# Order of the attention products in each unit, and the two ends of a spatial self-attention kernel

## The chip, the cores and the metric

The kernel runs on one core of a Trainium2 chip. The metric is the device time of one execution in microseconds (us). The kernel before takes 2449.17 us, the median of 10 executions (2448.07 to 2451.79).

## What is computed

The reference is self-attention over the 4096 positions of each of four images, with raw reshapes: the projections are made per position, and then the (position, channel) block of each image is read anew as (channel, position).

```
q = x @ Wq + bq        # x: (4, 64, 64, 256), q and k: 128 channels
k = x @ Wk + bk
v = x @ Wv + bv        # 256 channels
pq, pk, pv = reshape of q, k, v to (B, channels, N), N = 4096
energy = einsum('bcn,bcm->bnm', pq, pk)
attention = softmax(energy, axis=-1)
out = einsum('bcm,bnm->bcn', pv, attention)
y = gamma * out.reshape(x.shape) + x          # float32
```

## The kernel before

**Tiling.** Each image has 32 row blocks of 128 keys (`NM` = 32) and 16 groups of 256 queries (`NG` = 16). A group is worked off in eight units (`NU` = 8), and a unit holds four key blocks. So there are 4 x 16 x 8 = 512 units. In the loop at the end of the fast part, `u` counts an image's 128 units, and `g, t = divmod(u, NU)` gives the group and the unit's place `t` in it.

**Split numbers.** The products run on 32-bit tiles of the type float32r, and each factor is split into an upper part and rests, so that three products stand for one. For the energies (`energy`, L330) a unit has 12 products of 256 columns: 8 into `sa` and 4 into `sb`. ACT takes their exponentials into `x` and `y` (L334), DVE multiplies these (`join`, L344), ACT makes the upper part `h` (`upper`, L349), and DVE makes `l` and `d` (`halves`, L355 and L358). Then `attend` (L383) adds the unit's share of the output: `h` times `vh`, `l` times `vl`, `d` times `vd`, eight products for each pair, in this order. I call the three sets of eight **phases h, l and d**.

**The products of a phase.** The stationary operand is a block of the unit's own tile, `left[:, i, j * P : (j + 1) * P]`, with `i` = 0 to 3 for the key block and `j` = 0 or 1 for the half of the 256 queries. The moving operand is the value block `right[:, m, :]` with

```
m = 2 * t + i // 2 + NI * (i % 2)
```

that is `m` = 2t, 2t+16, 2t+1, 2t+17 for `i` = 0 to 3. In `vh` and `vl` a value block has 256 channels, two columns of ones that sum the softmax's denominator, and two columns of padding: the products move 258 columns, and the blocks lie 260 x 4 = 1040 bytes apart. In `vd` there are 256 columns, 1024 bytes apart. Phases h and l add into the PSUM tiles `a0` and `a1` (one for each `j`, each in a bank of its own), phase d into `bb` (both `j` in one bank). The order in a phase is `j` outermost and `i` inside, upwards; only in phase l, for `j` = 1 and `t` = 1 or 3, `i` runs downwards (`back`).

**Order of the work.** The schedule is written out by hand (`manual_schedule`): energies of unit u + 3, `join` and `upper` of u + 2, `halves` of u + 1, `attend` of u. So an engine's instructions run in the order in which the loop issues them. After the last unit of a group ACT copies the two sums out of PSUM (L394), and `finish` scales, transposes and adds `x` some units later. The next group's sums use the same PSUM tiles.

**The start.** ACT's queue issues the two loads of `Wq` and `Wk` (L90, L91) first; ACT then loads its activation table and writes the ones into `vh` and `vl` (L224). SP's queue loads the blocks of `x` (L82), POOL's queue the biases, `Wv`, `bv` and `gamma`. PE runs 12 transposes of the identity tile into a scratch tile `wp` (L199), whose result nobody reads; the identity tile is made by POOL. Then it transposes the first two blocks of `x` (L124) and projects the first (L137).

**The end.** `finish_last` handles the last group of the last image. DVE copies the two denominators (L447), `factors` takes reciprocals and multiplies by gamma (L399, L400), L450 makes the second factor; `guard` checks that all denominators lie in a safe range (L431 to L439), piece by piece between the other steps. For each half, ACT scales `bb` out of PSUM (L455), DVE adds the scaled sum to it (L458), PE transposes (L463), DVE adds `x` (L468), and SP stores (L469). The value that `guard` leaves in `again` decides whether a slower general version runs; in these executions it doesn't.

Of the kernel before, what the change touches and what calls it, by code (L numbers as in the profile page):

```python
# [9 lines left out]
F32 = mybir.dt.float32  # L10
F32R = mybir.dt.float32r
I32 = mybir.dt.int32
AF = mybir.ActivationFunctionType
ALU = mybir.AluOpType
AX = mybir.AxisListType
# [5 lines left out]
def kernel(  # L21
# [36 lines left out]
    nc = tc.nc  # L58
    B, W, H, C = x.shape
    P = 128  # L60
    N = W * H
    C2 = C // 2
    NM = N // P
    KC = C // P
    NI = NM // 2
# [19 lines left out]
    ident = const.tile([P, P], F32, name="ident")  # L85
    make_identity(nc, ident)
    ones = const.tile([P, P], F32, name="ones")
    nc.vector.memset(ones, 1.0)
    wqk_sb = const.tile([P, KC, 2 * C2], F32, name="wqk_sb")
    nc.scalar.dma_start(wqk_sb[:, :, :C2], wq.rearrange("(k p) d -> p k d", p=P))  # L90
    nc.scalar.dma_start(wqk_sb[:, :, C2:], wk.rearrange("(k p) d -> p k d", p=P))  # L91
    bqk_sb = const.tile([P, 2 * C2], F32, name="bqk_sb")
    nc.gpsimd.dma_start(bqk_sb[:, :C2], bq.partition_broadcast(P))
    nc.gpsimd.dma_start(bqk_sb[:, C2:], bk.partition_broadcast(P))
# [6 lines left out]
    gam, gam1 = gam2[:, :1], gam2[:, 1:]  # L101
# [73 lines left out]
    NB = 256  # L175
    NJ = NB // P
    NG = N // NB
    NU = NM // 4
# [3 lines left out]
    E = 2.0**-12  # L182
# [4 lines left out]
    again = const.tile([P, 1], I32, name="again")  # L187
    zs = const.tile([P, 1], F32, name="zs")

    zall = const.tile([P, B * NG, NJ], F32, name="zall")  # L190
# [4 lines left out]

    with tc.tile_pool(name="ps_w", bufs=1, space=PSUM) as ps_w:
        wp = ps_w.tile([P, P], F32, name="wp")
        for _ in range(12):
            nc.tensor.transpose(wp, ident, ident)  # L199

    with ExitStack() as fast:
        fast.enter_context(tc.manual_schedule())
# [6 lines left out]
        ppool = pool("ppool", 2)  # L209
        pool("pad2", 1).tile([P, 112], F32, name="pad2")  # L210
        work = pool("work", 2)
# [3 lines left out]
        ps_s = pool("ps_s", 2, space=PSUM)  # L215
        ps_o = pool("ps_o", 1, space=PSUM)
        ps_t = pool("ps_t", 1, space=PSUM)


        vh = qkv.tile([P, NM, VC], F32R, tag="vh", name="vh")  # L220
        vl = qkv.tile([P, NM, VC], F32R, tag="vl", name="vl")
        vd = qkv.tile([P, NM, C], F32R, tag="vd", name="vd")
        for t in (vh, vl):
            nc.scalar.copy(t[:, :, C : C + 2], ones[:, : 2 * NM].rearrange("p (m t) -> p m t", t=2))  # L224

        images, qd, kf, units, loads, now = [], {}, {}, {}, {}, {}

# [124 lines left out]
        def halves(b, u):  # L352
# [7 lines left out]
            )  # L360
            units[b, u] = h, l, d

        def attend(b, u):

            g, t = divmod(u, NU)
            if t == 0:
                now["acc"] = [
                    ps_o.tile([P, C + 2], F32, tag=f"a{j}", name=f"a{j}_{b}_{g}")
                    for j in range(NJ)
                ]  # L370
                now["bb"] = ps_o.tile([P, NJ, C], F32, tag="bb", name=f"bb_{b}_{g}")
            h, l, d = units[b, u]
            acc, bb = now["acc"], now["bb"]
            for left, right in ((h, vh), (l, vl), (d, vd)):
                for j in range(NJ):
                    out_ = bb[:, j, :] if left is d else acc[j]


                    back = left is l and j == NJ - 1 and t in (1, 3)
                    for i in reversed(range(4)) if back else range(4):  # L380
                        m = 2 * t + i // 2 + NI * (i % 2)

                        nc.tensor.matmul(  # L383
                            out_,
                            left[:, i, j * P : (j + 1) * P],
                            right[:, m, : out_.shape[1]],
                            start=(t == i == 0 and (left is h or left is d and j == 0)),
                            stop=(t == NU - 1 and i == 3 and left is not h),
                            skip_group_check=True,
                        )  # L390
            if t == NU - 1 and (b, g) != (B - 1, NG - 1):
                o = now["o"] = work.tile([P, NJ, C + 2], F32, tag="o", name=f"o_{b}_{g}")
                for j in range(NJ):
                    nc.scalar.activation(o[:, j, :], acc[j], AF.Identity, scale=1.0 + E)  # L394

        def factors(b, g, gamma):

            r = work.tile([P, 2, NJ], F32, tag="r", name=f"r_{b}_{g}")
            nc.vector.reciprocal(r[:, 0, :], zall[:, b * NG + g, :])  # L399
            nc.vector.tensor_tensor(r[:, 0, :], r[:, 0, :], gamma.to_broadcast([P, NJ]), ALU.mult)  # L400
            return r[:, 0, :], r[:, 1, :]

        def finish(b, g, o, bb, xr):
            yield
            yield

            nc.vector.tensor_copy(zall[:, b * NG + g, :], o[:, :, C])
            r, _ = factors(b, g, gam1)
            nc.vector.tensor_tensor(o[:, :, :C], o[:, :, :C], bb, ALU.add)
            yield  # L410
            for j in range(NJ):
                nc.scalar.activation(
                    o[:, j, :C], o[:, j, :C], AF.Identity, scale=r[:, j : j + 1]
                )
            yield
            yield
            tp = ps_t.tile([P, 2, NB], F32, tag="t", name=f"ot_{b}_{g}")
            for s in range(2):
                for j in range(NJ):
                    nc.tensor.transpose(  # L420
                        tp[:, s, j * P : (j + 1) * P], o[:, j, s * P : (s + 1) * P], ident
                    )
            yield
            nc.vector.tensor_tensor(xr, xr, tp, ALU.add)
            nc.gpsimd.dma_start(ov[b, g], xr)

        def guard():

            z = zall.rearrange("p n j -> p (n j)")
            ok = ppool.tile([P, 4, NB], F32, tag="y", name="ok")[:, 0, : B * NG * NJ]  # L430
            nc.vector.tensor_scalar(ok, z, Z_LOW, None, ALU.is_ge)  # L431
            nc.vector.scalar_tensor_tensor(ok, z, Z_HIGH, ok, ALU.is_le, ALU.mult)
            yield
            nc.vector.tensor_reduce(zs, ok, AX.X, ALU.min)
            nc.vector.tensor_scalar(zs, zs, 0.5, None, ALU.is_lt)
            zp = ps_s.tile([P, 1], F32, tag="b", name="zp")
            nc.tensor.matmul(zp, ones, zs, start=True, stop=True)
            yield
            nc.vector.tensor_copy(again, zp)  # L439
            yield  # L440
            yield

        def finish_last(b, g, xr):

            for j in range(NJ):
                a = now["acc"][j]
                nc.vector.tensor_copy(zall[:, b * NG + g, j : j + 1], a[:, C : C + 1])  # L447
            r, ra = factors(b, g, gam)
            check = guard()
            nc.vector.tensor_scalar(ra, r, 1.0 + E, None, ALU.mult)  # L450
            o = work.tile([P, NJ, C + 2], F32, tag="o", name=f"o_{b}_{g}")
            tps = []
            for j in range(NJ):
                next(check)
                nc.scalar.activation(  # L455
                    o[:, j, :C], now["bb"][:, j, :], AF.Identity, scale=r[:, j : j + 1]
                )
                nc.vector.scalar_tensor_tensor(  # L458
                    o[:, j, :C], now["acc"][j][:, :C], ra[:, j : j + 1], o[:, j, :C], ALU.mult, ALU.add
                )  # L460
                tp = (ps_t, ps_s)[j].tile([P, 2, P], F32, tag="ta"[j], name=f"ot_{b}_{g}_{j}")
                for s in range(2):
                    nc.tensor.transpose(tp[:, s, :], o[:, j, s * P : (s + 1) * P], ident)  # L463
                tps.append(tp)
            for j in range(NJ):
                next(check)
                n = slice(j * P, (j + 1) * P)
                nc.vector.tensor_tensor(xr[:, :, n], xr[:, :, n], tps[j], ALU.add)  # L468
            nc.sync.dma_start(ov[b, g], xr)  # L469
# [19 lines left out]
        for b in range(B):  # L489
            pr = images[b]  # L490
            if b == 0:
                now["banks"] = energies
                pr.transposed(0)
                pr.transposed(1)
                project_qk(b, 0)
            for i in range(1, NI):
# [13 lines left out]
            for u in range(STEPS):  # L510
                g, t = divmod(u, NU)
# [47 lines left out]
    NB = 512  # L559
    NG = N // NB  # L560
    NJ = NB // P
    NP = NM // 2
    xg, og = columns(x, NB), columns(out, NB)
    with tc.If(nc.values_load(again[0:1, 0:1]) > 0), ExitStack() as general:
# [4 lines left out]
        ppool, work = pool("gp", NP + 2), pool("gw", 1)  # L569
        ps_s = pool("gs", 2, space=PSUM)  # L570
        ps_t = pool("gt", 2, space=PSUM)
        ps_o = pool("go", 1, space=PSUM)
        for b in range(B):
# [16 lines left out]
            for g in range(NG):  # L590
                ps = []
                mx = work.tile([P, 2, NB], F32, tag="mx", name=f"gmx_{b}_{g}")
                for t in range(NP):
                    sp = ps_s.tile([P, 2, NB], F32, tag="s", name=f"gs_{b}_{g}_{t}")
                    for h in range(2):
# [4 lines left out]
                            start=True,  # L600
                            stop=True,
                        )
                    p = ppool.tile([P, 2, NB], F32, tag="p", name=f"gp_{b}_{g}_{t}")
# [7 lines left out]
                for j in range(NJ):  # L611
# [17 lines left out]
                acc = [  # L629
                    ps_o.tile([P, NB], F32, tag=f"o{s}", name=f"go{s}_{b}_{g}")  # L630
                    for s in range(2)
                ]
# [60 lines left out]
```

## Time and profile before

| | |
|---|---|
| median of 10 executions | 2449.17 us |
| the profiled execution | 2448.89 us |
| its span, first to last instruction | 2447.1 us |
| PE busy | 2434.0 us, 19,982 products |
| DVE busy | 2100.0 us |
| ACT busy | 1795.3 us |
| POOL busy | 424.6 us |
| DMA | 498.92 MB, mean 204 GB/s |

The profile is of one execution. PE is the engine of the matrix products, PEld its loads of the stationary operand, DVE the vector engine, ACT the engine of the activation functions, POOL the general one, SP the one that only issues transfers here. A line of a group of instructions gives the source line, the engine, the operation, the tiles (out<-in), the shapes, how many there were, their busy time, the mean length of one in ns, and the idle time ahead of them with what ended it. A product's length in the records is longer than the distance to the next one, because the products are pipelined; where I speak of the pace of products I use the distance from start to start.

### The profile page before, as it was taken

The numbers are of one execution on the slowest core, as the hardware profiler recorded it, in microseconds if no ns is written. First come the engines' busy times: TensorE is split into PE (matmuls) and PEld (weight loads), VectorE is DVE, ScalarE is ACT, GpSimd is POOL, SyncE is SP. The second block draws the span as 40 slices with busy tenths as digits, with TensorE's granted clock in tenths as the row PEclk, the third lists the DMA queues.
The fourth block names the chain that finished last, engine by engine and source line by source line (L and its number), as shares of the span: only waits on it lengthen the run. The fifth ranks groups of instructions, "written<-read, shape, count | busy, mean of one in ns | idle before, by whom it ended". The sixth has DMA issues, their size and how long they took to land.

```text
span 2447.1 us, 50024 instructions
## 1 busy us (share of the span) xinstructions
PE 2434.0 (99%) x19982; PEld 2403.2 (98%) x19982; DVE 2100.0 (86%) x2314; ACT 1795.3 (73%) x3201; POOL 424.6 (17%) x781
## 2 busy tenths in 40 slices
PE   9999999999999999999999999999999999999998
PEld 8999999999899999999989999999998999999998
DVE  5988888888698888888869888888886988888887
ACT  5777777777677777777667777777766777777775
POOL 4211111111411111111141111111114111111110
PEclk9999999999999999999999999999999999999999
DMA  7766666665776666666477666666647766666663
GB/s 232 221 203 212 205 205 201 205 213 157 231 224 198 209 206 206 207 198 212 145 241 228 202 203 206 206 211 201 206 141 246 227 204 201 206 207 211 203 202 112
DMA packets 137407, 498.92 MB, mean 204 GB/s; under 512 B 15536, under 2 KB 57264, under 8 KB 137168
## 3 DMA queue, kind: packets, MB, share of 16 engines
q0 software_dynamic: 92320, 453.17, 59.6%
q1 hardware_dynamic: 44304, 42.22, 5.5%
q8 instruction: 160, 2.62, 0.4%
q14 instruction: 79, 0.65, 0.1%
q10 hardware_dynamic: 544, 0.26, 0.0%
HBM read 445.25 MB, written 50.33 MB: 203 GB/s over the span
## 4 chain that ended last, share of the span: by engine, by line


## 5 line engine op out<-in xcount | busy, mean ns | idle before, releaser
L334 ACT ACTIVATE x<-sa 128x512 f32<-128x512 f32 x1024 | 612.3, 598 | 510.2 <-PE sa L330 508.0
L344 DVE TENSOR_TENSOR x<-x,y 128x1024 f32<-128x1024 f32 x512 | 626.9, 1224 | 228.4 <-ACT y L334 228.4
L330 PE MATMUL sa<-q,k 128*128 128x256 f32 x4096 | 733.6, 279 | 0.0
L358 DVE SCALAR_TENSOR_TENSOR d<-h,x 128x1024 fp32r<-128x1024 f32 x512 | 624.3, 1219 | 0.0
L355 DVE TENSOR_TENSOR l<-x,h 128x1024 fp32r<-128x1024 f32 x512 | 624.0, 1219 | 0.0
L330 PEld LDWEIGHTS sa<-q,k 128*128 128x128 f32 x4096 | 618.1, 188 | 0.7 <-ACT y L334 0.2
L334 ACT ACTIVATE y<-sb 128x512 f32<-128x512 f32 x1024 | 616.2, 602 | 0.0
L383 PE MATMUL a<-vh,h 128*128 128x258 f32 x4096 | 574.6, 283 | 0.0
L383 PE MATMUL a<-vl,l 128*128 128x258 f32 x4096 | 572.2, 282 | 0.0
L330 PE MATMUL sb<-q,k 128*128 128x256 f32 x2048 | 567.2, 277 | 0.0
L383 PE MATMUL bb<-vd,d 128*128 128x256 f32 x4096 | 556.7, 278 | 0.0
L314 POOL DMA_DIRECT2D k<-kf x512 | 278.8, 545 | 1568.1 <-PE sb L330 1535.7
L349 ACT ACTIVATE h<-x 128x1024 fp32r<-128x1024 f32 x512 | 544.2, 1063 | 8.6 <-DVE x L344 8.0
L383 PEld LDWEIGHTS a<-vl,l 128*128 128x128 f32 x4096 | 524.6, 189 | 0.0
L383 PEld LDWEIGHTS a<-vh,h 128*128 128x128 f32 x4096 | 522.8, 190 | 0.0
L383 PEld LDWEIGHTS bb<-vd,d 128*128 128x128 f32 x4096 | 513.6, 188 | 0.0
L330 PEld LDWEIGHTS sb<-q,k 128*128 128x128 f32 x2048 | 385.1, 188 | 0.1
L137 PE MATMUL qk<-wqk_sb,xts 128*128 128x256 f32 x512 | 121.1, 379 | 0.0
L158 PE MATMUL v<-xts,wv_sb 128*128 128x256 f32 x512 | 120.3, 380 | 0.0
L158 PEld LDWEIGHTS v<-xts,wv_sb 128*128 128x128 f32 x512 | 97.5, 190 | 13.0
L137 PEld LDWEIGHTS qk<-wqk_sb,xts 128*128 128x128 f32 x512 | 92.5, 190 | 9.8
L275 POOL DMA_DIRECT2D qd<-qks x128 | 69.3, 549 | 179.5 <-DVE qks L146 170.3
(56 smaller groups left out, 865.3 us busy)
## 6 DMA issues: line engine op xcount, KB each, us to landing
k<-kf POOLq DMA_DIRECT2D x512, 768.0 KB, 4.6
x<-in_x_dram SPq DMA_DIRECT2D x128, 256.0 KB, 3.9
kf<-f POOLq DMA_DIRECT2D x64, 384.0 KB, 3.9
out_dram<-x POOLq DMA_DIRECT2D x63, 256.0 KB, 2.6
qd<-qks POOLq DMA_DIRECT2D x128, 64.0 KB, 2.9
qr<-qd SPq DMA_DIRECT2D x64, 128.0 KB, 3.6
wv_sb<-in_L_conv_Wv_dram POOLq DMA_DIRECT2D x1, 256.0 KB, 6.7
out_dram<-x SPq DMA_DIRECT2D x1, 256.0 KB, 3.6
```

Source lines behind the costliest of these rows:

```text
L137: nc.tensor.matmul(qk[:, s, :], self.xt[i][:, k, s, :], wqk_sb[:, k, :], start=(k == 0), stop=(k == KC - 1),)
L158: nc.tensor.matmul(vp[:, eh, :], wv_sb[:, k, eh * P : (eh + 1) * P], self.xt[i][:, k].rearrange("p s a -> p (s a)"), start=(k == 0), stop= ...
L275: nc.gpsimd.dma_start(qd[b, i // 2 + NG // 2 * s][:, i % 2, :], x[:, s, :C2])
L314: nc.gpsimd.dma_start(t.rearrange("p (i s) f d -> p i s (f d)", s=2), kf[b, u % NU])
L330: nc.tensor.matmul(to[:, i], kt[:, 2 * k + i, f, :], q[:, f], start=first, stop=last)
L334: nc.scalar.activation(to[:, 2 * k : 2 * k + 2, :], sp.rearrange("p i j d -> p i (j d)"), AF.Exp, scale=scale,)
L344: nc.vector.tensor_tensor(x, x, y, ALU.mult)
L349: nc.scalar.activation(h, units[b, u], AF.Identity, scale=UPPER)
L355: nc.vector.tensor_tensor(l, x, h.bitcast(F32), ALU.subtract)
L358: nc.vector.scalar_tensor_tensor(d, h.bitcast(F32), 1.0 + E, x, ALU.mult, ALU.subtract)
L383: nc.tensor.matmul(out_, left[:, i, j * P : (j + 1) * P], right[:, m, : out_.shape[1]], start=(t == i == 0 and (left is h or left is d and ...
```

## The change

It has four parts.

1. The two loads of `Wq` and `Wk` are issued by ACT's queue after the two writes of ones into `vh` and `vl`, and so after the table load.
2. PE's idle products at the start are 7 plain products of the tile of ones (which DVE writes with a memset) in place of 12 transposes of the identity; and 2 more stand between the transposes of the first and the second block of `x`.
3. In phases h and l the eight products run in an order that a table gives for each `t` and phase; a digit is 4j + i. Phase d runs as before, `01234567`. The flag `start`, which begins a sum in a PSUM bank, is set at the first product into each bank, whichever it is.
4. In `finish_last` ACT scales the sums out of `a0` and `a1`, each with its own factor, and DVE adds the scaled `bb`; before, it was the other way round. The range check of all but the last group's denominators is done ahead, that of the last group's two after their factors, and `again` is written with a comparison between the two halves. `factors` and `guard` are gone; `finish` has the lines of `factors` in it.

```diff
-    nc.scalar.dma_start(wqk_sb[:, :, :C2], wq.rearrange("(k p) d -> p k d", p=P))
-    nc.scalar.dma_start(wqk_sb[:, :, C2:], wk.rearrange("(k p) d -> p k d", p=P))
...
-        for _ in range(12):
-            nc.tensor.transpose(wp, ident, ident)
+        for _ in range(7):
+            nc.tensor.matmul(wp, ones, ones, start=True, stop=True)
...
         for t in (vh, vl):
             nc.scalar.copy(t[:, :, C : C + 2], ones[:, : 2 * NM].rearrange("p (m t) -> p m t", t=2))
+        nc.scalar.dma_start(wqk_sb[:, :, :C2], wq.rearrange("(k p) d -> p k d", p=P))
+        nc.scalar.dma_start(wqk_sb[:, :, C2:], wk.rearrange("(k p) d -> p k d", p=P))
...
+        ORDERS = (
+            ("13564072", "14325076"),
+            ("41256307", "41763502"),
+            ("26147053", "35601472"),
+            ("41236075", "57104632"),
+            ("10436572", "10726543"),
+            ("57164203", "34250167"),
+            ("35042176", "65341027"),
+            ("35210467", "15347062"),
+        )
+
+        def order(f, b, g, t):
+            return "01234567" if f == 2 else ORDERS[t][f]
...
-            for left, right in ((h, vh), (l, vl), (d, vd)):
-                for j in range(NJ):
+            begun = set()
+            for f, (left, right) in enumerate(((h, vh), (l, vl), (d, vd))):
+                for n, x in enumerate(order(f, b, g, t)):
+                    j, i = divmod(int(x), 4)
                     out_ = bb[:, j, :] if left is d else acc[j]
-                    back = left is l and j == NJ - 1 and t in (1, 3)
-                    for i in reversed(range(4)) if back else range(4):
-                        m = 2 * t + i // 2 + NI * (i % 2)
-                        nc.tensor.matmul(
-                            out_,
-                            left[:, i, j * P : (j + 1) * P],
-                            right[:, m, : out_.shape[1]],
-                            start=(t == i == 0 and (left is h or left is d and j == 0)),
-                            stop=(t == NU - 1 and i == 3 and left is not h),
-                            skip_group_check=True,
-                        )
+                    bank = 2 if left is d else j
+                    m = 2 * t + i // 2 + NI * (i % 2)
+                    nc.tensor.matmul(
+                        out_,
+                        left[:, i, j * P : (j + 1) * P],
+                        right[:, m, : out_.shape[1]],
+                        start=(t == 0 and bank not in begun),
+                        stop=(t == NU - 1 and n >= 6 and left is not h),
+                        skip_group_check=True,
+                    )
+                    begun.add(bank)
...
+        def inside(ok, z):
             nc.vector.tensor_scalar(ok, z, Z_LOW, None, ALU.is_ge)
             nc.vector.scalar_tensor_tensor(ok, z, Z_HIGH, ok, ALU.is_le, ALU.mult)
...
+            inside(ok[:, 0, :n0], z[:, :n0])
+            nc.vector.tensor_reduce(last[:, NJ:], ok[:, 0, :n0], AX.X, ALU.min)
+            acc, bb = now["acc"], now["bb"]
+            for j in range(NJ):
+                zj, raj = z[:, n0 + j : n0 + j + 1], r[:, 1, j : j + 1]
+                nc.vector.tensor_copy(zj, acc[j][:, C : C + 1])
+                nc.vector.reciprocal(r[:, 0, j : j + 1], zj)
+                nc.vector.tensor_tensor(raj, r[:, 0, j : j + 1], gam1, ALU.mult)
+                nc.scalar.activation(o[:, j, :C], acc[j][:, :C], AF.Identity, scale=raj)
+            nc.vector.tensor_tensor(r[:, 0, :], r[:, 0, :], gam.to_broadcast([P, NJ]), ALU.mult)
+            inside(last[:, :NJ], z[:, n0:])
+            nc.vector.tensor_reduce(zs, last, AX.X, ALU.min)
             zp = ps_s.tile([P, 1], F32, tag="b", name="zp")
             nc.tensor.matmul(zp, ones, zs, start=True, stop=True)
             tps = []
             for j in range(NJ):
                 nc.vector.scalar_tensor_tensor(
-                    o[:, j, :C], now["acc"][j][:, :C], ra[:, j : j + 1], o[:, j, :C], ALU.mult, ALU.add
+                    o[:, j, :C], bb[:, j, :], r[:, 0, j : j + 1], o[:, j, :C], ALU.mult, ALU.add
                 )
...
+                if j == 0:
+                    nc.vector.tensor_scalar(again, zp, P - 0.5, None, ALU.is_lt)
...
                 pr.transposed(0)
+                wp = ps_t.tile([P, P], F32, tag="t", name="wp1")
+                for _ in range(2):
+                    nc.tensor.matmul(wp, ones, ones, start=True, stop=True)
                 pr.transposed(1)
```

## Prediction

> **What bounds the kernel now.** I read the page's head first, then the groups of instructions, then the timeline of one unit, of the last unit, of the first 9 us and of the last 4.
>
> ```profile
> PE 2434.0 (99%) x19982; PEld 2403.2 (98%) x19982; DVE 2100.0 (86%) x2314; ACT 1795.3 (73%) x3201; POOL 424.6 (17%) x781
> PEclk9999999999999999999999999999999999999999
> ```
>
> PE has no gaps to speak of and its clock is full in every slice. So the time is the number of products times their pace, and the ends. DVE is next, with 14% to spare.
>
> ```profile
> L330 PE MATMUL sa<-q,k 128*128 128x256 f32 x4096 | 733.6, 279 | 0.0
> L383 PE MATMUL a<-vh,h 128*128 128x258 f32 x4096 | 574.6, 283 | 0.0
> L383 PE MATMUL a<-vl,l 128*128 128x258 f32 x4096 | 572.2, 282 | 0.0
> L383 PE MATMUL bb<-vd,d 128*128 128x256 f32 x4096 | 556.7, 278 | 0.0
> L344 DVE TENSOR_TENSOR x<-x,y 128x1024 f32<-128x1024 f32 x512 | 626.9, 1224 | 228.4 <-ACT y L334 228.4
> ```
>
> No group of products has idle time ahead of it. DVE even waits 228.4 us for ACT, and ACT in turn for PE's energies: both follow PE. One unit in the timeline (columns: start, length, engine):
>
> ```profile
> 401.38 0.39 PE L330 MATMUL sa<-q,k 128*128 128x256 f32 x2
> ...
> 402.74 1.12 PE L383 MATMUL a<-vh,h 128*128 128x258 f32 x8
> 403.70 1.12 PE L383 MATMUL a<-vl,l 128*128 128x258 f32 x8
> 404.65 1.09 PE L383 MATMUL bb<-vd,d 128*128 128x256 f32 x8
> 405.58 0.39 PE L330 MATMUL sa<-q,k 128*128 128x256 f32 x2
> ```
>
> Twelve energies take 1.36 us from start to start (113.3 ns each), phase h 0.96, l 0.95, d 0.93: 4.20 us a unit. 512 units are 2150 us of the 2447. Two columns more than 256 should cost 2/256 of 113.3, 0.9 ns, so 114.2 ns a product; h and l take 119.6. The last unit, with nearly all else at rest, goes at the same pace:
>
> ```profile
> 2433.71 1.13 PE L383 MATMUL a<-vh,h 128*128 128x258 f32 x8
> 2434.67 1.12 PE L383 MATMUL a<-vl,l 128*128 128x258 f32 x8
> 2435.63 1.08 PE L383 MATMUL bb<-vd,d 128*128 128x256 f32 x8
> ```
>
> So the 5.4 ns above 114.2 come from PE and its own operands, not from DVE, ACT or a transfer. I then took the starts of the single products from the trace, over some 50 repeats of each `t`. A place in the order repeats to about 1 ns, and the places differ widely: 113 to 125 ns. Four products in a row (one `j`) take 478.2 ns on the mean, 468.3 at best (t = 6, l, second four), 488.3 at worst (t = 6, h, second four); a phase takes 956.4, from 944.1 to 973.3. The same `m`, `j` and order give different times in h and l, and I found no rule by `m`, `i` or the product before that foretells them. After such a phase the first one to four products of d are slow too: the first seven take 803 to 817 ns, and 817 for t = 1, 4 and 5.
>
> **What the Trainium skill says.** "TensorE: Matmul & The Clock Gate", section "Back-to-back issue gap": in a stream of weight loads and products the spacing is set by both. The trace fits: 128 columns of weights and 256 of data show 113.3 ns, and only the data's width and place differ in h and l. The same page, "Step-by-step: what each phase is for", says that loading the next weights takes no read bandwidth from the running product; the aligned d phase at 113.3 agrees, the h and l phases have an extra that no page I read explains or prices, nor is a change of PSUM bank between products priced. The same page, "What's actually happening": the clock is halved until PE has been busy for about 3.4 us. The trace agrees in kind: the idle transposes start 213 ns apart, those of the second block of x 109. "Trainium Kernel Development and Optimization", "Key Constraints": transfers of all queues share 16 engines; so moving two loads frees others only for as long as those bytes take.
>
> **Part 3, the orders.** 8192 products of h and l, 1024 phases, are put in other orders. Number, size and operands stay. Bounds per phase: at best all at 114.2, 8 x (119.6 - 114.2) = 43 ns gained; at worst all fours like the worst seen, 2 x 10.1 = 20 ns lost. In between: all fours like the best seen gain 2 x 9.9 = 20 ns, all phases like the best seen 12.3. The profile can't say which kind of draw the 16 lists are; I found no rule to price them by. I take the middle of the two "best seen" figures, 16 ns, because each of the 16 lists is its own choice where before one order served all eight `t`, with their eight different address offsets, so that no list has to serve for a place that it is bad for; that is a judgement, not a reading. 1024 x 16 = 16.4 us. With other history ahead of d, its first seven may take 805 to 807 for t = 1, 4, 5 as for most: 11 x 3/8 = 4 ns a unit, 2.1 us; bounds -1 to +4 us of gain, I take 2. Is there a new limit at once? A unit falls by 0.036 us to 4.16. DVE needs 2100/512 = 4.10 us a unit over the whole span, projections included; in the unit quoted it needs three operations of 1.22, 3.67 us. It is near but not reached. A unit of 4.10 is about where the gain would stop: 51 us of gain, beyond my lower end. What waits for the order: ACT's copies of the two sums (L394) start in this trace after both are done (413.42, after the l phase), and the next h phase starts 1.9 us later (415.34), so the sum of `j` = 0 ending later costs nothing; without that cover it would cost 0.48 us a group. **Sum: 18.5 us gained.**
>
> **Parts 1 and 2, the start.**
>
> ```profile
> 0.73 0.42 ACTq L90 DMA_DIRECT2D wqk_sb<-in_L_conv_Wq_dram  x1
> 1.70 1.28 ACT L224 ACT_TABLE_LOAD   x1 [1.70 <-PEq L678]
> 2.43 2.82 PE L199 MATMUL wp<-ident 128*128 128x128 f32 x12 [2.43 <-POOL ident masks.py:199]
> 5.31 1.12 PE L124 MATMUL xt<-ident,x 128*128 128x128 f32 x4
> 7.84 0.66 PE L124 MATMUL xt<-ident,x 128*128 128x128 f32 x4 [1.41 <-DMA x<-in_x_dram]
> 8.34 1.89 PE L137 MATMUL qk<-wqk_sb,xts 128*128 128x256 f32 x8
> ```
>
> The last wait of the start is for the second block of x, at 7.84. The weights (issued 0.73 and 1.18, 2.2 and 3.3 us to land) are there by 4.5. Moved behind the table load (which starts about 1 us sooner without the two issues) and the two writes, they are issued at about 2.5 and 3.0 and land near 5 to 6.5, still ahead of 8.34. Their 256 KB leave the engines free for x early (1.0 us at the 260 GB/s of 2 to 4 us), but come back before the second block is in. So 0 to 1.0 us gained; I take 0.5. The idle products no longer wait for POOL: from about 1.0 instead of 2.43, 7 x 0.213 = 1.5 us, so the first block's transposes start when it lands; that gains nothing while the second block is the last to come. Risk: PE now rests between 2.5 and the first block, and again before the second, so the clock may come late. In this trace it is full by 7.84; if it came only after 3.4 us of work from there, half of that would be lost, 1.7 us, at most 3.4. Bounds of the start: 1.0 gained to 3.4 lost; I take 0.3 gained.
>
> **Part 4, the end.**
>
> ```profile
> 2436.75 0.84 ACT L455 ACTIVATE o<-bb,r 128x256 f32<-128x256 f32 x2 [6.73 <-PE bb L383]
> 2437.26 0.48 DVE L458 SCALAR_TENSOR_TENSOR o<-a,r,o 128x256 f32<-128x256 f32 x1 [0.22 <-ACT o L455]
> 2438.04 0.47 DVE L458 SCALAR_TENSOR_TENSOR o<-a,r,o 128x256 f32<-128x256 f32 x1
> 2438.74 0.75 DVE L468 TENSOR_TENSOR x<-x,ot 128x256 f32<-128x256 f32 x2
> ```
>
> ACT's two scalings (0.47 each) leave the path behind `bb`, as the sums are ready with the l phase, near 2435.8. But DVE now has ten small operations before its first L458: two chains of three, the product with gamma, two of the check and a reduction, at 0.2 us where one needs the one before, 0.1 else: 1.5 to 2.0, so 2437.3 to 2437.8 against 2437.26. The second L458 no longer waits for the reduction of 128 values and follows `again`, at 2437.95 to 2438.5 against 2438.04. The end moves by between 0.2 gained and 0.4 lost; I take 0.
>
> **Sum.** 18.5 + 0.3 + 0 = 18.8 from the profiled execution's 2448.89 (span 2447.1 and 1.8 around it): 2430.1. It lies 0.28 under the median, so 2430.4 for the median; I say 2430.
>
> **The rivals.** A, **the order doesn't matter on the mean**: slow and quick places only change seats (a product of 123 to 125 ns is often followed by one of 114 to 116), and 478 per four stays. For it: the means of the phases lie within 1.5% of each other but for one. Against it: the outliers of 468 and 488. Then only d and the ends move: 2449.2 - 1 = 2448. B, **a change of accumulator costs**: the lists change `j` 69 times in 16 phases, 4.3 a phase, before once. In the trace the product after the change takes 119.0 ns, the one before 118.2, against 119.6 in all: no cost is seen; its worst is 125. At 5.5 ns each, 3.3 x 1024 x 5.5 = 18.6 us: 2467. From 1.6 ns a change (5.4 us, the ends taken off) it ends slower by more than 0.2%.
>
> **Chances.** A measurement of this kernel can tell about 0.2%, 4.9 us, from no change. The forecast, fewer ns per product, 0.75; A 0.14; B 0.11. The range reaches from 2411 (a gain of 38 us, most of the 43 ns a phase) to 2448, where A ends; what is left out is B and a little below.
>
> **What would show it.** The mean of the two `vh` and `vl` groups falls by about 2 ns (283 and 282 to 281 or 280), phase starts 0.94 us apart, a unit of 4.16; the d group falls by under 1; energies stay. With A the means stay; with B they rise to 286. At the start, product L137's first start within 1 us of 8.34; at the end, from the last `bb` phase's start (2435.63) to SP's last issue (2439.52) within 0.4 of 3.89 us. The prediction is wrong if the h and l pace falls and the unit doesn't, because DVE or ACT ends last.

## The result, and the profile after

The changed kernel takes 2439.52 us, the median of 8 executions (2437.30 to 2441.03), against 2449.74 for the kernel before in the executions beside them (28, 2448.02 to 2451.79). The ratio is 0.9958, with an interval of 0.995 to 0.9967: 10.2 us faster. The profiled execution took 2440.59 us, its span is 2438.8. The head of its page and the groups of products and of DVE's first product:

```profile
span 2438.8 us, 50041 instructions
...
PE 2426.1 (99%) x19988; PEld 2394.8 (98%) x19988; DVE 2100.2 (86%) x2318; ACT 1797.6 (74%) x3201; POOL 424.5 (17%) x781
...
L344 DVE TENSOR_TENSOR x<-x,y 128x1024 f32<-128x1024 f32 x512 | 627.1, 1225 | 217.8 <-ACT y L334 217.8
L330 PE MATMUL sa<-q,k 128*128 128x256 f32 x4096 | 733.3, 279 | 0.0
...
L398 PE MATMUL a<-vh,h 128*128 128x258 f32 x4096 | 569.6, 281 | 0.0
L398 PE MATMUL a<-vl,l 128*128 128x258 f32 x4096 | 568.8, 281 | 0.0
...
L398 PE MATMUL bb<-vd,d 128*128 128x256 f32 x4096 | 553.0, 277 | 0.0
```

The mean of the `vh` group fell from 283 to 281 ns, that of `vl` from 282 to 281, that of `bb` from 278 to 277; the energies stayed at 279. PE is still without a gap, and DVE still waits for ACT (217.8 us, before 228.4), so no new bound arose. The same unit as the one shown of before (t = 5), on PE:

```profile
404.47 1.12 PE L398 MATMUL a<-vh,h 128*128 128x258 f32 x8
405.43 1.10 PE L398 MATMUL a<-vl,l 128*128 128x258 f32 x8
406.37 1.09 PE L398 MATMUL bb<-vd,d 128*128 128x256 f32 x8
407.30 0.39 PE L330 MATMUL sa<-q,k 128*128 128x256 f32 x2
```

From start to start: h 0.96, l 0.94, d 0.93 us. This unit is one of those that gained little. The starts of the single products give this in ns (before / after; the median over the repeats of each `t`, from a phase's first start to the next start of another kind):

| t | h | l | d |
|---|---|---|---|
| 0 | 957 / 948 | 956 / 962 | 921 / 917 |
| 1 | 958 / 951 | 952 / 945 | 937 / 924 |
| 2 | 955 / 946 | 953 / 951 | 918 / 910 |
| 3 | 951 / 941 | 957 / 946 | 919 / 907 |
| 4 | 954 / 950 | 956 / 950 | 930 / 913 |
| 5 | 957 / 955 | 952 / 942 | 930 / 930 |
| 6 | 973 / 949 | 944 / 942 | 916 / 916 |
| 7 | 963 / 948 | 963 / 951 | 920 / 921 |
| mean | 958.7 / 948.5 | 954.2 / 948.4 | 923.9 / 917.2 |

By these medians a unit gains 10.1 + 5.7 + 6.7 = 22.5 ns. One median hides two cases: after the change phase h of `t` = 2 takes 946 ns in 36 of the 64 groups and 964 in the other 28. Over all units the means fall by 8.7 (h), 5.8 (l) and 6.9 ns (d), so a unit gains 21.4 ns, 11.0 us for 512.

The 28 groups are the same ones in both kernels: every second group of an image from the fourth on. In them ten of the twelve energies ahead of `t` = 2 run 117.8 ns apart in place of 113.3, after the four transposes of `finish` (L420 before, L431 after), and phase h starts from that other pace. The order of the products and the value blocks are the same in all 64 groups. So what a list takes depends also on what runs just before it.

Cut at the first start of the first and of the last phase h, the two spans fall into three stretches:

| stretch | before | after | gained |
|---|---|---|---|
| start, up to the first phase h | 75.39 us | 78.75 us | -3.36 |
| from there to the last phase h | 2358.31 | 2347.28 | 11.03 |
| from there to the end | 13.41 | 12.78 | 0.63 |

The middle stretch repeats well: two more traces with the old order have 2357.91 and 2357.99, four more with the new one 2347.21 to 2347.39. So the loop gained 11, and this execution's start gave 3.4 of it back, measured against the start in the profile of before. The timeline of the start, and a table of its stretches (columns: the stretch, its length, busy time of PE, PEld, DVE, ACT and POOL with counts, granted clock, share of the DMA engines, GB/s):

```profile
1.03 0.44 ACTq L223 DMA_DIRECT2D wqk_sb<-in_L_conv_Wq_dram  x1
...
1.05 3.18 PE L197 MATMUL wp<-ones 128*128 128x128 f32 x14 [1.05 <-DVE ones L88]
...
4.37 0.63 PE L122 MATMUL xt<-ident,x 128*128 128x128 f32 x4
...
4.83 0.61 PE L508 MATMUL wp<-ones 128*128 128x128 f32 x4
...
8.39 1.11 PE L122 MATMUL xt<-ident,x 128*128 128x128 f32 x4 [2.95 <-DMA x<-in_x_dram]
...
9.30 3.62 PE L135 MATMUL qk<-wqk_sb,xts 128*128 128x256 f32 x8
```

```profile
6.00:8.00 2.00, 0.00 (x0) 0.00 (x0) 0.00 (x0) 0.00 (x0) 0.00 (x0) 0.83 0.82 222
8.00:10.00 2.00, 1.61 (x6) 1.52 (x7) 0.00 (x0) 0.46 (x1) 0.00 (x0) 0.50 0.74 247
10.00:12.00 2.00, 2.00 (x6) 1.55 (x6) 0.00 (x0) 0.13 (x1) 0.45 (x2) 0.50 0.45 138
12.00:14.00 2.00, 2.00 (x9) 1.62 (x8) 0.69 (x1) 0.32 (x1) 0.05 (x1) 0.50 0.01 3
14.00:16.00 2.00, 2.00 (x10) 1.79 (x9) 0.97 (x3) 0.57 (x2) 1.64 (x3) 0.96 0.33 80
```

PE's clock was full early: the first block's transposes took 0.63 us. But PE rested for 2.95 us until the second block of `x` was in at 8.39 (7.84 before). By the trace's clock records it went to half at 7.33 and came back at 14.16. Work from 8.39 to 14.16 went at half pace: half of 5.77 is 2.9 us, and 0.55 for the later block: 3.4, by this estimate the whole difference between the two profiles. How typical the start of before was is taken up with the experiments. The end:

```profile
2428.78 0.88 ACT L459 ACTIVATE o<-a,r 128x256 f32<-128x256 f32 x2 [6.37 <-DVE zall L456]
...
2429.75 0.48 DVE L468 SCALAR_TENSOR_TENSOR o<-bb,r,o 128x256 f32<-128x256 f32 x1
...
2430.43 0.48 DVE L468 SCALAR_TENSOR_TENSOR o<-bb,r,o 128x256 f32<-128x256 f32 x1
...
2431.43 0.42 DVE L479 TENSOR_TENSOR x<-x,ot 128x256 f32<-128x256 f32 x1 [0.20 <-PE ot L473]
```

The last phase d starts at 2427.93, so the two L468 start 1.82 and 2.50 us after it; before, the two L458 started 1.63 and 2.41 after theirs. The chain is 0.1 to 0.2 us longer, and yet the stretch to the end of the span is 0.6 us shorter. The experiments say why.

### The profile page after: what moved, and what is told of

It reads as the page before. It is cut to its first block, busy times and chain, and to the rows that moved or that the text cites. A ratio compares the mean times of both kernels' runs of the same rounds, so it can differ in the third digit from the quotient of the medians.

```text
span 2438.8 us, 50041 instructions
## 1 busy us (share of the span) xinstructions
PE 2426.1 (99%) x19988; PEld 2394.8 (98%) x19988; DVE 2100.2 (86%) x2318; ACT 1797.6 (74%) x3201; POOL 424.5 (17%) x781
## 4 chain that ended last, share of the span: by engine, by line
PE 99%; DMA 0%; DVE 0%; SPq 0%; issue 0%
PE a L398 40%; PE bb L398 19%; PE sa L330 19%; PE sb L330 10%; PE qk L135 5%; PE v L156 5%; PE xt L122 1%; PE ot L431 1%; DMA x<-in_x_dram 0%; SPq L82 0%; DVE o L468 0%; PE ot L473 0%; DVE x L479 0%; PE zp L465 0%; DVE r L457 0%
## 5 line engine op out<-in xcount | busy, mean ns | idle before, releaser
L344 DVE TENSOR_TENSOR x<-x,y 128x1024 f32<-128x1024 f32 x512 | 627.1, 1225 | 217.8 <-ACT y L334 217.8
```

Source lines behind the costliest of these rows:

```text
L344: nc.vector.tensor_tensor(x, x, y, ALU.mult)
```

## Experiments

My theory after the result: the orders are the whole gain; the lists gain because each is a good one for its place, owing to the way in which width and distance of the moved blocks disturb PE's pace; the start loses what the halved clock costs. The rivals: the mixing as such gains; a change of accumulator costs, and hides a larger gain; the ends gave part.

### The parts alone

**Orders alone.** The kernel before with part 3.

> The kernel before with part 3 alone (the tables of orders). My theory: the orders are the whole gain, 22 ns a unit as the two traces show (h 10, l 6, d 7), 512 x 0.022 = 11.3 us, and the start of the kernel before is kept, so 2438.5 us, 0.9954 of before. The rival, that the ends gave part of it, expects 2441 or more. A third, that the orders only gain together with a later start, expects no change.

```diff
-                    back = left is l and j == NJ - 1 and t in (1, 3)
-                    for i in reversed(range(4)) if back else range(4):
...
+                for n, x in enumerate(order(f, b, g, t)):
+                    j, i = divmod(int(x), 4)
```

Measured: 2437.82 us against 2450.34, ratio 0.9950 (0.9936 to 0.9963). The loop takes 2347.39 us, as in the changed kernel (2347.28), and the stretch to the end 13.39, as before (13.41). The orders are the gain.

**The ends alone.** The changed kernel with the old order.

> The changed kernel with the old order in its phases (parts 1, 2 and 4 alone). My theory: the start loses what the clock loses, 0 to 3.4 us by the execution, because PE rests 3 us ahead of the second block of x and the clock is halved again; the end gives nothing: 2450 to 2453 us, 1.0005 of before in the median. The prediction's step (0.3 us gained) expects 2449.4.

```diff
-            return "01234567" if f == 2 else ORDERS[t][f]
+            return "01237654" if f == 1 and t in (1, 3) else "01234567"
```

Measured: 2449.77 against 2450.34, ratio 0.9997 (0.9989 to 1.0006): no difference that can be told. In its trace the start loses 2.4 us against the profile of before (first phase h at 77.76) and the end gains 1.08 (12.33 against 13.41), which I had not expected. It is more than the 0.63 of the changed kernel: in the old order the sum of `j` = 0 is complete half way through phase l, and ACT can start on it.

**Work for PE between the two blocks.** The changed kernel with 14 idle products in place of 2.

> The changed kernel with 14 idle products in place of 2 between the first two blocks of x, so that PE has work until the second block lands. If the lost clock is the cause of the late start, PE is at full clock from its first release on, the second block's transposes take 0.6 us in place of 1.1, phase h of the first unit starts 2.5 to 3 us sooner than in the changed kernel's profile, and the time is 2437 us. If the late landing of the second block is the cause (0.55 us later than before), the time stays within 1 us of the changed kernel's 2439.5.

```diff
-                for _ in range(2):
+                for _ in range(14):
                     nc.tensor.matmul(wp, ones, ones, start=True, stop=True)
```

Measured: 2438.20 against 2450.34, ratio 0.9952 (0.9938 to 0.9965); the five times lie within 1.2 us (2437.72 to 2438.93), where the changed kernel's spread over 3.7. Its start:

```profile
4.51 1.09 PE L122 MATMUL xt<-ident,x 128*128 128x128 f32 x4
5.39 3.71 PE L508 MATMUL wp<-ones 128*128 128x128 f32 x28
8.94 0.60 PE L122 MATMUL xt<-ident,x 128*128 128x128 f32 x4
9.37 1.89 PE L135 MATMUL qk<-wqk_sb,xts 128*128 128x256 f32 x8
```

The second block's transposes take 0.60 in place of 1.11 us and the projection's eight records 1.89 in place of 3.62: the clock stays full, and the first phase h comes 2.3 us sooner than in the changed kernel's profile. So the lost clock is the cause of most of the late start in that profile. In the median it is less than I expected, 1.3 us. The changed kernel seems not to lose the clock every time: of its ten executions, the two with a mean clock of 0.999 took 2437.3 and 2437.5 us, the eight with 0.998 took 2439.2 to 2441.2. The 14 products here end a little late (8.94).

The start of before is no fixed measure either. Ten traces of this document have it, that of the kernel before among them, and reach the first phase h at 75.0 to 78.2 us, 76.7 on the mean. In the three at 75.0 to 75.6 the clock was full by 6.8 us and stayed so. In six it became full only between 10.6 and 13.7 us, and in one it fell back to half at 9.07. So the profile of before (75.39) shows one of the good starts. Against the mean of the ten the changed kernel's trace is late by 2.1 us, not 3.4.

**Orders and end, with the start of before.**

> The changed kernel without parts 1 and 2: orders and end are new, the start is that of before. My theory: 2438.5 us like the orders alone, with the end worth nothing (0.2 gained to 0.4 lost). If the end gains from the scaling being taken off the path, it is 0.3 to 0.6 us under the orders alone.

```diff
-        for _ in range(7):
-            nc.tensor.matmul(wp, ones, ones, start=True, stop=True)
+        for _ in range(12):
+            nc.tensor.transpose(wp, ident, ident)
```

(and the two loads of the weights ahead of the table load again, and no products between the blocks). Measured: 2437.29 against 2450.34, ratio 0.9951 (0.9938 to 0.9965): 0.5 us under the orders alone, about what the traces' ends say (12.76 against 13.39), though the times of the two overlap.

### What the orders do

**Good lists at the wrong place.**

> The kernel before with the 16 lists of the changed kernel, each used at the next t (the list of t + 1 at t). If the lists are good for their place alone, the phases h and l go back to the mean of before, 956 ns, or to any draw between 944 and 973; the time is near 2449. If it is the mixing as such that gains (any mixed order), h and l stay near 948.5 and the time near 2438.5.

```diff
+        def order(f, b, g, t):
+            return "01234567" if f == 2 else ORDERS[(t + 1) % NU][f]
```

One execution took 2457.18 us, against 2448.72. The same lists, one place on, make the loop 6.9 us longer (2365.18 against 2358.31) where at their own place they take 11 off it; the rest of the difference is the start. Phase h takes 956.6 ns on the mean and l 958.5: what the plain order takes. So it isn't the mixing as such; a list is good or bad for its place, which means its addresses and also the products around it, since the neighbouring lists moved with it. The loss I had not expected: at t = 3 phase d takes 944 ns in place of 919, and the twelve energies after it 1413 in place of 1360.

**A change of accumulator at every product.**

> The kernel before with one order for all h and l phases, 04152637: the accumulator changes at every product, and each value block is moved twice in a row. If a change of accumulator costs (the rival of the prediction, 1.6 to 5.5 ns each, 7 a phase against 1), a phase takes 966 to 990 ns and the time is 2454 us or more. My theory, no cost of the change as such: 940 to 970 ns by the place, mean within 6 of 956.

```diff
+            return "01234567" if f == 2 else "04152637"
```

One execution took 2464.75 us, against 2448.72. It is slower by 16 us, 13.9 of them in the loop (2372.17), yet not by the rival's mechanism. The groups of its PE:

```profile
L387 PE MATMUL a<-vl,l 128*128 128x258 f32 x4096 | 575.1, 282 | 0.0
L387 PE MATMUL a<-vh,h 128*128 128x258 f32 x4096 | 574.4, 283 | 0.0
...
L387 PE MATMUL bb<-vd,d 128*128 128x256 f32 x4096 | 561.1, 279 | 0.0
```

h and l have the means of before, 283 and 282; d rose from 278 to 279. From the starts, h takes 959 ns (0.5 more than before) and l 960.5 (6 more), where 1.6 ns for each of six more changes would have been 10 and 5.5 ns 33. The rest is in d (933 against 924) and in energies at 1413 ns in two of the eight units. A price of the change as such falls. This order also moves each value block twice in a row, which might have hidden a price, but the other traces give none: over the places within phases h and l of five orders (this one, the old one, the upward one, and the 16 lists at their own place and shifted), at the 282 places after a change a product starts 119.4 ns after the one before it on the mean, at the 278 others 119.6.

**No downward runs.**

> The kernel before without its two downward runs (01234567 in all h and l phases). My theory: only the l phases of t = 1 and 3 and what comes right after them change, by up to 15 ns each; the time moves by under 2 us. If the downward runs were worth 8.6 ns per four as a comparison within those units suggests, the two phases take 960 and 965 ns and the time rises by 1.1 us.

```diff
+        def order(f, b, g, t):
+            return "01234567" if f == 2 else "01234567"
...
-                    back = left is l and j == NJ - 1 and t in (1, 3)
-                    for i in reversed(range(4)) if back else range(4):
```

One execution took 2455.91 us, against 2448.72: 7.2 us slower, where I expected under 2. The two l phases take 960 ns, near what the comparison said (952 and 957 before). The large part comes after them. The unit t = 3, PE's timeline:

```profile
397.94 1.12 PE L387 MATMUL a<-vl,l 128*128 128x258 f32 x8
398.90 1.11 PE L387 MATMUL bb<-vd,d 128*128 128x256 f32 x8
399.85 0.40 PE L330 MATMUL sa<-q,k 128*128 128x256 f32 x2
...
401.26 0.40 PE L387 MATMUL a<-vh,h 128*128 128x258 f32 x2
```

d takes 0.95 us from start to start and the energies 1.41, where the energies of before took 1.36. In the single starts the products of d come 117.5 or 118.3 ns apart from the third on, not 113.3, and the energies of the next unit go on so. PE has a second steady pace, 117.8, that it can fall into after a phase l and here keeps through 8 + 12 products with 256 columns, until the next phase h. Per group of eight units, as means over the groups, phases l and d of t = 1 lose 13 ns, those of t = 3 lose 33, and the energies ahead of t = 4 lose 53. Ahead of t = 2 there is a gain of 18: here only 4 of the 64 groups have the slow pace there, before it was 28. With 2 ns elsewhere that is 83 ns a group, 5.3 us for 64; the loop is 5.2 us longer (2363.53 against 2358.31), and the start 1.8.

**Width and distance of the moved blocks.** Three versions of the kernel before in which phase l alone differs.

> The kernel before with 256 columns moved in phase l in place of 258, from the same places; it leaves out the rests' share of the softmax's denominators. If the width of 258 causes the 5.4 ns above pace, phase l takes 907 ns and the time falls by 24 us. If the blocks' distance of 1040 bytes causes it, phase l stays within 10 ns of 954 and the time within 6 us.

```diff
-                            out_,
+                            out_[:, :C] if left is l else out_,
...
-                            right[:, m, : out_.shape[1]],
+                            right[:, m, : (C if left is l else out_.shape[1])],
```

> The kernel before with the value rests of phase l 1024 bytes apart in place of 1040 and 256 columns moved in place of 258 (leaves out the rests' share of the softmax's denominators). With 256 columns at 1040 bytes phase l took 944 ns, 10 less than before. If the distance makes the rest of the excess, phase l now goes like phase d: 907 to 935 ns, its first products slow after h, the others 113.3. If the distance has no part in it, phase l stays at 944.

```diff
-        vl = qkv.tile([P, NM, VC], F32R, tag="vl", name="vl")
+        vlf = qkv.tile([P, NM * VC], F32R, tag="vl", name="vl")
+        vl = vlf[:, : NM * C].rearrange("p (m c) -> p m c", c=C)
...
-                            out_,
+                            out_[:, :C] if left is l else out_,
...
-                            right[:, m, : out_.shape[1]],
+                            right[:, m, : min(out_.shape[1], right.shape[2])],
```

> The same distance of 1024 bytes with 258 columns (the last two are the next block's first two, so the denominators get a wrong small share). If the width of 258 alone upsets the pace, phase l takes 930 to 960 ns in spite of equal offsets; if the distance alone does, it takes 914 (113.3 + 0.9 a product) to 935.

(with the tile `vlf` as in the version above)

```diff
-                            right[:, m, : out_.shape[1]],
+                            vlf[:, m * C : m * C + C + 2] if left is l else right[:, m, : out_.shape[1]],
```

Phase l took, on the mean over `t` of the medians:

| | 1040 bytes apart | 1024 bytes apart |
|---|---|---|
| 258 columns | 954 ns (before) | 968 |
| 256 columns | 944 | 927 |

The times are 2451.40 against 2448.72 (256 columns, 1040 bytes), 2436.30 against 2450.40 (256, 1024) and 2459.15 against 2450.40 (258, 1024); the loops take 2358.97, 2343.01 and 2368.33 us against 2358.31. Neither of the two is the cause by itself: 258 columns upset the pace at the distance of 1024 bytes too, and even more, beyond what I had expected of either cause; and with 256 columns at 1024 bytes phase l goes as d does, at 113.3 from the third to the fifth product on, but for t = 1 and t = 3, which fall into 117.8. With the distance the address at which each block begins changes too; the two were not separated. The group of l in that version, beside its h:

```profile
L384 PE MATMUL a<-vh,h 128*128 128x258 f32 x4096 | 575.0, 283 | 0.0
...
L384 PE MATMUL a<-vl,l 128*128 128x256 f32 x4096 | 558.1, 279 | 0.0
```

283 against 279 in one execution. The first of these versions gained 10 ns a phase in l and nothing in the loop, since the slow pace came up elsewhere: in the energies after t = 5 (1413 ns), and after t = 2 in 28 of 64 groups, and in d at t = 0, 2, 5 and 7 (5 to 10 ns on the mean).

### The end, and a mended start

**The flag written early.** The kernel before with its check ahead of the last steps.

> The kernel before with its range check run ahead of the last group's steps (it leaves out the last group's denominators), so that the flag is written about 1.5 us sooner. My theory: after the flag POOL goes through a closing step of 6.7 us that ends last, so the stretch from the last phase d's last product to the end of the span falls from 10.68 us to 9.5 to 9.8, though the store is issued at the same time or at most 0.3 us sooner. If the store's landing sets the end, the stretch falls only by as much as the store's issue moves.

```diff
+            z = zall.rearrange("p n j -> p (n j)")[:, : (B * NG - 1) * NJ]
...
+            for _ in guard():
+                pass
             for j in range(NJ):
                 a = now["acc"][j]
...
-            check = guard()
...
-                next(check)
```

One execution took 2449.28 us, against 2450.40. From the last phase d's last product to the end of the span it takes 10.13 us in place of 10.68. That is 0.55 less, though DVE's steps queued behind the flag and the store was issued 0.5 us later after that product (3.58 in place of 3.08). So the store doesn't set the end. POOL's closing steps, as the views of the kernel's last line give them, for the kernel before, the changed one, and this one (length in ns, smallest, middle, largest; first and last start):

```profile
L689 POOLq DRAIN  x3: 46/107/6683, 2439.6 to 2446.8; - x3
```

```profile
L704 POOLq DRAIN  x3: 46/107/6683, 2431.3 to 2438.5; - x3
```

```profile
L688 POOLq DRAIN  x3: 46/107/6683, 2438.6 to 2447.1; - x3
```

The step of 6.683 us starts when POOL has read the flag `again` and passed the branch on it. In the kernel before that is 3.15 us after the last product's start (2436.44), in the changed one 2.53 (2428.74), in this one 1.36 (2437.29). Where it starts 0.62 sooner, in the changed kernel, the end comes 0.61 sooner. In this version it comes off the path, and SP's closing steps after the store end last; so the gain stops at 0.55. My figure of 9.5 to 9.8 us overlooked that DVE's steps would be queued behind the flag.

**All parts with the start mended.**

> All parts with the start mended: orders and end of the changed kernel, loads of the weights first as before, 7 idle products of ones, 6 more between the two first blocks of x, and upward order in phase l of the last unit so that the sum of j = 0 is ready early. Against the changed kernel: 1 to 3.4 us at the start (second block 0.5 us sooner, clock not lost), 0.4 us at the end: 2436 to 2437, under the 2437.3 of orders and end with the old start. If the clock is still lost in most runs, 2438.

```diff
+            last = (b, g, t) == (B - 1, NG - 1, NU - 1)
+            return "01234567" if f == 2 or f == 1 and last else ORDERS[t][f]
...
+                for _ in range(6):
+                    nc.tensor.matmul(wp, ones, ones, start=True, stop=True)
```

Measured: 2437.23 against 2450.40 (2436.04 to 2437.60 in five), ratio 0.9946 (0.9933 to 0.996). In its trace the clock was full from 6.59 us on and stayed so, and the end is 9.57 us after the last product's start, against 10.07 in the changed kernel, from the sum of `j` = 0 being ready early; the old order with the new end has the same 9.6. It is some 2 us under the changed kernel, and cannot be told from orders and end with the start of before (2437.29).

## Why the prediction was right, and where its sizes were off

The prediction has the right sign and the right place of the gain, and 2439.52 lies within its range; the gain of 10.2 us is about half of the 19 foretold. The sign was not read from the profile. It rested on the judgement that the lists were good draws, and the same lists one place on made the loop 6.9 us longer; so there was luck in it. By its own steps:

- **What bounds it.** Right: PE's pace and the ends. DVE waited nearly as long as before, and no new wait took the place of the gain.
- **The extra time in h and l comes from PE and its own operands.** Shown for phase l: width and distance of the moved blocks, with the same order and the same work on the other engines but for the writing of these blocks, shift it between 927 and 968 ns. What in PE does it stays open; I found no rule that foretells a place. Two readings of the trace were too even: a place does not always repeat to 1 ns (at t = 2 the two kinds of groups differ by up to 6 ns in a place already before), and the phases but one lie within 2.0% of each other, not 1.5.
- **16 ns a phase.** This is the term that was mis-sized. Over all units it measured 8.7 in h and 5.8 in l, 7.3 on the mean: 7.4 us for 1024 phases, not 16.4. I had put it between two "best seen" figures, of which the lower, 12.3, already asked every phase to be like the best of 16. The best phase after takes 941 ns, and the mean, 949, lies about half way from the mean of before, 956.6, to that. My reason, a list of its own for each place, does not make a better draw: the experiment with shifted lists shows that these lists are fitted to their places, and that one place on they aren't better than the plain order.
- **4 ns a unit in d.** It measured 6.9, 3.5 us in place of 2.1; t = 1 and 4 became quicker as expected, t = 5 did not, and t = 0, 2 and 3 did, which I had not counted. The mechanism, what l leaves behind, was right, but I took it to be over after one to four products. The slow pace that can last through d and the next energies was not in my list of cases. It is the largest single effect of an order that the runs showed (29 ns in d and 53 in the energies at t = 3 without the downward runs), and an order that falls into it would have made the change slower. At t = 3 the kernel before is kept free of it by its downward run, and the changed one is free of it there as well. Neither is free of it altogether: in both, the energies ahead of t = 2 run at the slow pace in 28 of 64 groups.
- **The start, 0.3 gained.** Against the profile of before it lost 3.4 us, the far end of my bounds; against the mean of ten traces with the start of before 2.1. In the times the loss is smaller or not clear: loop and end gained 11.7 us by the traces and the medians 10.2, which leaves some 1.5 us, and the ends alone show no loss that can be told. Two steps failed. I priced an idle product at 0.213 us from the transposes; a plain float32 product of 128 columns is two records of 0.213 at half clock (14 records for 7), as the 3.18 us show. It did no harm. And the rest ahead of the second block was named as a risk, but I valued it at only 0.2 us (0.5 less 0.2 is the 0.3), and I read "full by 7.84" from one trace as if each execution did so. The earlier landing of the second block wasn't seen either: the second block's transposes began at 8.39 and 8.52 us in the two traces with the later weights where nothing else held them back, and from 7.47 to 8.33 in eleven traces with the weights first. That leans to a loss of some 0.5 us, but I ran no test of the loads alone.
- **The end, 0.** It gained 0.6, from the flag, which I had only looked at as one more step on DVE; POOL's closing step of 6.683 us behind it was not on my path. The chain to the store went as estimated: 0.06 us longer (3.14 after the last product's start, 3.08 before).
- **Rivals.** A, no effect on the mean, falls: 12.5 us for the orders alone, 10.9 in the loop. B, a price for the change of accumulator, falls as a mechanism; that a bad order can be 16 us slower holds.

## What to carry to other kernels

When PE is busy in every slice, look at the starts of single products: the pace of equal products can vary by 10% with width, place and order, and an order is good only at its place, with its addresses and the products before and after it, so a table of orders has to be measured where it is used. Take the best place already seen as the far end of such a gain, not as the middle of the forecast. Compare a start of some microseconds over several traces, since one trace can show a lucky one. At a start that waits for a load, keep PE at work until the load lands; and ask of the end which engine's closing steps it waits for, not only when the last store is issued.

## What the runs showed of the hardware that was not expected

- **Two steady paces.** Products of 256 columns follow each other 113.3 ns apart, or 117.8 once upset, for up to 20 products on end. Without the downward runs the order of PE's own products set it off; in 28 of 64 groups of both kernels it comes after four transposes. What decides it stays open.
- **The clock fell after a shorter rest than I reckoned with.** "TensorE: Matmul & The Clock Gate", section "HAM oscillation — how this bites in real kernels", warns of gaps over some 3.4 us. Here PE had ended its work at 5.44 and the clock was halved at 7.33 us, in a gap of 2.95 us. In the kernel before, a gap of 1.41 us did no harm, but in the trace with the order `04152637` the clock was lost after one of 2.05 us: it was halved at 9.07, with PE at work again since 8.17.
- **The clock changes in steps of 3.413 us.** In the clock records of all these traces full and halved stretches between two changes last whole multiples of 3.413 us: in the changed kernel's trace 3.41 full and 6.83 halved, with the ends alone and with `04152637` 3.41 and 3.41, and in the kernel before the long full stretch of 2433.70 us is 713 steps. Where a step begins differs from execution to execution, and so the same start can come out well or badly. By an estimate from PE's busy time in these steps, the full clock was lost after steps in which PE was busy for 26 to 41% (three traces), and kept after the steps of 54% and more around the same gap (five traces). In these eight the gaps of the lost ones are also the longer ones (2.05 to 2.95 us, against 1.65 and less), so the runs don't tell the busy share of a step from the length of the gap.
- **POOL's closing step of 6.683 us** is the same in all fourteen traces, and starts when POOL has passed the last branch; with 10.7 us from the last product to the end, it is most of that stretch.
